# Two graph-attention layers on one core: moving head, value and residual work between VectorE, ScalarE and TensorE

## The chip, the cores and the metric

The kernel runs on one core of a Trainium2 chip. The metric is the device time of one execution in microseconds. Five engines work beside each other, each through its own instruction stream in its own order, and wait for one another by semaphores: TensorE (PE; its weight loads are listed apart as PEld), VectorE (DVE), ScalarE (ACT), GpSimd (POOL) and SyncE (SP), which here only issues transfers.

## The reference, cut to what matters

Sixteen graphs (batches) of N = 1024 nodes with D = 256 features go through two layers; everything is fp32.

```python
# layer 0: 4 heads of 64. With a 0/1 adjacency only edge type 1 exists.
h = x @ W                                   # 4 heads x 64
w = leaky_relu(e_src[i] + e_dst[j]);  w = -1e9 where adj == 0
dst = softmax(w) @ h + bias
out = relu(dst) + h                         # per head
out = (out - mean) / sqrt(var + 1e-6) * ln_gamma + ln_beta   # over the 64 of a head
x = layernorm(x + out)
# layer 1: 8 heads of 32
n = layernorm(x) * gamma1 + beta1
o = softmax(where(adj > 0, n n^T / sqrt(32), -inf)) @ n
x1 = x + o;  y = layernorm(x1) * gamma2 + beta2
x = layernorm(x1 + gelu(y @ W1 + b1) @ W2 + b2)              # 256 -> 1024 -> 256
```

## The kernel before, in words

A batch's 1024 nodes are 8 blocks of 128 rows (`NB`), or two halves of 512 (`NH`, `BPH` = 4 blocks each). Two Python generators, `layer0` and `layer1`, each run over all batches and yield after every step with a cost. A loop at the end of `fast_path` decides which of them makes the next step: `COURSE` says how far layer 0 of the next batch should be while layer 1 of this batch is at a given place, so that layer 0 of batch b+1 is woven into layer 1 of batch b. All of it is decided when the program is built.

Layer 0 of a batch is `prepare` and then `attention0`. `prepare` goes over pairs of blocks: it transposes x (L253), transposes the adjacency (L321) into an 8-bit mask (L322), multiplies x by the weights into a PSUM tile `ph` of 264 columns (L348), and takes from it on ScalarE the exponentials of the attention terms (L349 to L351) and four products of 128x64 that are the values `v0` (L353), and on VectorE the residual `hb` = `ph` + bias (L373). `attention0` has 16 steps a batch: VectorE makes four 128x512 weight tiles (L400), TensorE multiplies them by the values (L415) into an accumulator `av` in PSUM; every two steps one head of one half is complete. The last column of `av` is the softmax's denominator.

`after0` is a chain, a generator whose pieces are given out later, when a clock of step costs reaches them (`begin(chain, wait)`, and `yield` inside the chain for the next wait). `complete(chain)` gives out all that remains at once. For each head the chain divides, applies the ReLU and adds the residual (L444, L447, L456). After the fourth head of a half it does the four heads' norms together on tiles of 128x1024 (L471 to L487, with a square on ScalarE, L477, and a power on GpSimd, L224), then the row norm and layer 1's first norm (`sq` at L240), the residual `x1` (L510), the transposed normed rows `nT` (L253, L259) and the values `v1` (L520). Layer 1's attention needs `nT` and `v1` of both halves.

Layer 1 of a batch is `attention1`, 32 steps of four heads each (scores L543, exponentials L548, mask L554, products with the values L561 and L568), and then `mlp`: per 256 rows eight hidden blocks (L663, GELU at L670), and for each 128 rows the second product (`second`, L676, 16 recorded matmuls in one stretch), followed by the last norm (L706 on). `finish1` stands between the two: it adds the residual, makes the norm and adds `b2` to `x1` (L638, L639).

PSUM has 8 tiles in rotation: four `ps` (scores, hidden blocks, spread factors), two `acc` (`ps_a`: `ph`, `av`, and transposes through `side_bank` while layer 1 is in its attention), two `po`.

Of the kernel before, what the change touches and what calls it, by code (L numbers as in the profile page):

```python
# [39 lines left out]
P = 128  # L40
# [10 lines left out]
def fast_path(  # L51
# [55 lines left out]
    ps_a = ctx.enter_context(tc.tile_pool(name="ps_a", bufs=2, space=PSUM))  # L107
# [63 lines left out]
    for i, (_, _, dst) in enumerate(terms):  # L171
# [10 lines left out]
    nbias0_r = const.tile([P, D], F32, name="nbias0_r")  # L182
    nc.vector.tensor_scalar(nbias0_r, bias0_r, -1.0, None, op0=OP.mult)

    lng0_r, lnb0_r, g1_r, be1_r, b2_r = [
        const.tile([P, D], F32, name=name) for name in ("lng0_r", "lnb0_r", "g1_r", "be1_r", "b2_r")
# [6 lines left out]
    def later_weights():  # L193
        for t, src in ((lng0_r, lng0), (lnb0_r, lnb0), (g1_r, gamma1), (be1_r, beta1), (b2_r, b2)):
            nc.sync.dma_start(t, bass.AP(tensor=src.tensor, offset=src.offset, ap=[[0, P], [1, D]]))
# [7 lines left out]

        nc.vector.tensor_sub(b2_r, b2_r, be1_r)
# [36 lines left out]

    def side_bank(shape):

        if place[1][1] < ATTN1:
            return ps_a.tile(shape, F32, name="acc")
        return ps_s.tile(shape, F32, name="ps")
# [65 lines left out]
    def prepare(b, hb, esr, v0, dinv, mask):  # L312
# [3 lines left out]
        def turn_mask(k):  # L316
            i = b * NB + k
            ak = adj_blocks.pop(i)
            pt = ps_a.tile([P, NB, P], BF16, name="acc")
# [12 lines left out]
        for k in range(0, NB, GB):  # L332
# [12 lines left out]
            for g in range(GB):  # L345
                ph = ps_a.tile([P, D + 2 * H0], F32, name="acc")
# [5 lines left out]
                for hd in range(H0):  # L352
                    nc.scalar.mul(  # L353
                        v0[:, k + g, hd, 0:HO], ph[:, hd * HO : (hd + 1) * HO], v0[:, k + g, hd, HO : HO + 1]
                    )
                begin(take_h(hb[-1][:, (k + g) % BPH, :], ph), 1.5)
# [8 lines left out]
    def turn_sources(dst):  # L365
        es = ps_a.tile([P, GB, P], F32, name="acc")
        for g in range(GB):
            nc.tensor.transpose(es[:, g, :], apart[g].rearrange("p h q -> p (h q)"), ident)
        nc.scalar.copy(dst, es.rearrange("p g q -> p (g q)"))
        yield from ()  # L370

    def take_h(h, ph):
        nc.vector.tensor_add(h, ph[:, 0:D], bias0_r)  # L373
        yield from ()

    def attention0(b, hb, v0, esr, dinv, factors, mask, rinv):
# [51 lines left out]
        for i, (n, hd, j4) in enumerate(steps):  # L428
            if j4 == 0:
                av = ps_a.tile([P, BPH, HO + 1], F32, name="acc")  # L430
# [6 lines left out]
            if j4 == NB - 4:  # L437
                norms[b, n, hd] = after0(b, n, hd, av, hb[n], rinv[:, n * BPH : (n + 1) * BPH, :])
                begin(norms[b, n, hd], 2.5)
            yield 2.0  # L440

    def relu_residual(av, hd, hb, rinv):

        nc.vector.reciprocal(rinv[:, :, hd], av[:, :, HO])  # L444
        t = two.tile([P, BPH, HO], F32, name="relu")
        for q in range(BPH):
            nc.vector.scalar_tensor_tensor(  # L447
                t[:, q, :],
                av[:, q, 0:HO],
                rinv[:, q, hd : hd + 1],  # L450
                nbias0_r[:, hd * HO : (hd + 1) * HO],
                op0=OP.mult,
                op1=OP.max,
            )
        h = hb[:, :, hd * HO : (hd + 1) * HO]
        nc.vector.tensor_add(h, h, t)  # L456

    def after0(b, n, hd, av, o, rinv):


        relu_residual(av, hd, o, rinv)
        if hd < H0 - 1:
            return
        yield 1.5
        heads = [P, BPH * H0, HO]
        rowwise = [P, BPH, D]
        xl = one.tile(rowwise, F32, name="xl")
        load_x(xl, b, n * BPH, BPH)
        oh = o.rearrange("p g (h e) -> p (g h) e", e=HO)
        s = small.tile([P, BPH * H0], F32, name="s0")  # L470
        nc.vector.tensor_reduce(s, oh, axis=mybir.AxisListType.X, op=OP.add)  # L471
        nc.vector.scalar_tensor_tensor(
            oh, s[:, :, None].to_broadcast(heads), -1.0 / HO, oh, op0=OP.mult, op1=OP.add
        )
        yield 2.0
        sq = one.tile(rowwise, F32, name="sq")
        nc.scalar.activation(sq, o, AF.Square)  # L477
        yield 2.5
        v = small.tile([P, BPH * H0], F32, name="v0s")
        nc.vector.tensor_reduce(v, sq.rearrange("p g (h e) -> p (g h) e", e=HO), axis=mybir.AxisListType.X, op=OP.add)  # L480
        nc.vector.tensor_scalar(v, v, 1.0 / HO, EPS_HEAD, op0=OP.mult, op1=OP.add)
        r = power(v, BPH * H0, "r0")
        nc.vector.tensor_mul(o, o, lng0_r[:, None, :].to_broadcast(rowwise))
        nc.vector.tensor_add(xl, xl, lnb0_r[:, None, :].to_broadcast(rowwise))
        yield 3.0
        nc.vector.tensor_mul(oh, oh, r[:, :, None].to_broadcast(heads))
        nc.vector.tensor_add(o, o, xl)  # L487
        yield 2.0
# [17 lines left out]
        yield 2.5  # L506

        x1 = three.tile(rowwise, F32, name="x1")
        for g in range(BPH):
            nc.vector.scalar_tensor_tensor(  # L510
                x1[:, g, :], normed[:, g, :], ratio[:, g : g + 1], be1_r, op0=OP.mult, op1=OP.add
            )
        nT = two.tile([P, DC, HALF], F32, name="nT")
        for g in range(0, BPH, GB):
            transpose_rows(nT[:, :, g * P : (g + GB) * P], normed[:, g : g + GB, :], g1_c, be1_c)
            yield 1.5
        v1 = three.tile([P, BPH, H1, HD + 1], F32, name="v1")
        nc.vector.memset(v1[:, :, :, HD], 1.0)
        for g in range(BPH):
            nc.vector.tensor_mul(  # L520
                v1[:, g, :, 0:HD],
# [723 lines left out]
```

## Time and profile before

| | |
|---|---|
| time, median of 3 | 3648.02 us (3647.32 to 3652.49) |
| profiled span | 3649.4 us |
| PE busy | 3449.4 us, 95% |
| DVE busy | 2988.7 us, 82% |
| ACT busy | 2155.9 us, 59% |
| POOL busy | 384.4 us, 11% |
| first scores of the sixth batch to those of the seventh | 1022.92 to 1247.72 us |

Busy time is the union of an engine's instructions. Matmuls are pipelined and their ends are modelled, so a busy PE may still be a PE that is held up inside a run of matmuls. An fp32 matmul is recorded as two instructions, an fp32 transpose as one. One batch takes about 223 us, of which layer 1's attention takes some 134 us and its MLP some 89 us.

### The profile page before, as it was taken

The numbers are of one execution on the slowest core, as the hardware profiler recorded it, in microseconds if no ns is written. First come the engines' busy times: TensorE is split into PE (matmuls) and PEld (weight loads), VectorE is DVE, ScalarE is ACT, GpSimd is POOL, SyncE is SP. The second block draws the span as 40 slices with busy tenths as digits, with TensorE's granted clock in tenths as the row PEclk, the third lists the DMA queues.
The fourth block names the chain that finished last, engine by engine and source line by source line (L and its number), as shares of the span: only waits on it lengthen the run. The fifth ranks groups of instructions, "written<-read, shape, count | busy, mean of one in ns | idle before, by whom it ended". The sixth has DMA issues, their size and how long they took to land.

```text
span 3649.4 us, 142033 instructions
## 1 busy us (share of the span) xinstructions
PE 3449.4 (95%) x64417; PEld 2302.3 (63%) x64417; DVE 2988.7 (82%) x5332; ACT 2155.9 (59%) x4732; POOL 384.4 (11%) x360
## 2 busy tenths in 40 slices
PE   6699999999999999999999999999999999999998
PEld 5457576675756757566584765757567575665846
DVE  5788887888878888798887978888788887888884
ACT  3564746647475573755738466474664747557464
POOL 0102011010110101101010010101101011010110
PEclk9899999999999999999999999999999999999999
DMA  4100201011020110201102010020201102010000
GB/s 105 35 16 26 36 12 40 13 30 32 14 43 10 34 27 15 44 9 36 23 16 46 8 42 15 26 36 13 41 11 31 31 14 46 7 38 9 15 7 14
DMA packets 77814, 97.55 MB, mean 27 GB/s; under 512 B 9104, under 2 KB 60048, under 8 KB 77200
## 3 DMA queue, kind: packets, MB, share of 16 engines
q0 software_dynamic: 18432, 33.56, 6.5%
q1 hardware_dynamic: 57184, 53.76, 4.8%
q8 instruction: 506, 8.29, 0.9%
q10 hardware_dynamic: 1584, 1.05, 0.1%
q14 instruction: 108, 0.88, 0.1%
HBM read 105.13 MB, written 16.78 MB: 33 GB/s over the span
## 4 chain that ended last, share of the span: by engine, by line
PE 64%; DVE 25%; issue 4%; ACT 3%; POOL 3%; DMA 1%; SPq 0%; ACTq 0%; POOLq 0%; DVEq 0%
PE ps L543 13%; PE po L561 10%; PE ps L663 9%; PE acc L415 9%; DVE p L554 7%; PE po L676 7%; PE po L568 6%; DVE p L400 6%; PE acc L348 3%; POOL r L224 3%; DVE st L229 2%; PE acc L321 1%; PE acc L253 1%; PE ps L389 1%; DVE mv L230 1%
## 5 line engine op out<-in xcount | busy, mean ns | idle before, releaser
L554 DVE TENSOR_TENSOR p<-p,mask 128x1024 f32<-128x1024 f32 x1024 | 1199.3, 1218 | 161.2 <-ACT p L548 157.3
L548 ACT ACTIVATE p<-ps 128x512 f32<-128x512 f32 x2048 | 1059.6, 614 | 331.7 <-PE ps L543 329.9
L543 PE MATMUL ps<-nT 32*128 32x512 f32 x4096 | 770.1, 655 | 12.6 <-ACT cb L391 10.0
L400 DVE SCALAR_TENSOR_TENSOR p<-cb,dinv,mask 128x512 f32<-128x512 f32 x1024 | 698.5, 744 | 0.9 <-ACT cb L391 0.9
L568 PEld LDWEIGHTS po<-v,p 128*32 128x32 f32 x32768 | 389.4, 109 | 335.0 <-issue 239.3
L415 PE MATMUL acc<-v,p 128*64 128x65 f32 x16384 | 556.1, 226 | 42.1 <-DVE p L400 40.1
L415 PEld LDWEIGHTS acc<-v,p 128*64 128x64 f32 x16384 | 512.0, 139 | 114.3 <-DVE p L400 61.6
L670 ACT ACTIVATE hid<-ps,b_sb 128x256 f32<-128x256 f32 x512 | 235.5, 471 | 556.9 <-PE ps L663 556.5
L561 PE MATMUL po<-p,v 128*32 128x512 f32 x2048 | 548.3, 610 | 10.5 <-DVE p L554 8.8
L561 PE MATMUL po<-p,unit 128*32 128x512 f32 x2048 | 547.9, 610 | 0.0
L663 PE MATMUL ps<-yT,w_sb 128*128 128x256 f32 x2048 | 491.0, 387 | 0.4 <-issue 0.4
L676 PE MATMUL po<-w_sb,hid 128*128 128x256 f32 x2048 | 465.0, 381 | 0.0
L676 PEld LDWEIGHTS po<-w_sb,hid 128*128 128x128 f32 x2048 | 385.4, 190 | 64.0 <-issue 11.4
L663 PEld LDWEIGHTS ps<-yT,w_sb 128*128 128x128 f32 x2048 | 375.6, 190 | 64.9 <-issue 13.1
L568 PE MATMUL po<-v,p 128*32 128x33 f32 x32768 | 387.7, 198 | 9.5 <-issue 4.3
L543 PEld LDWEIGHTS ps<-nT 32*128 32x128 f32 x4096 | 268.2, 186 | 171.1 <-issue 56.9
L561 PEld LDWEIGHTS po<-p,v 128*32 128x32 f32 x2048 | 78.6, 109 | 388.3 <-DVE p L554 206.1
L224 POOL TENSOR_TENSOR r<-v,mhalf 128x1 f32<-128x1 f32 (+1 forms) x160 | 158.1, 988 | 1009.1 <-DVE v L710 721.6
L348 PE MATMUL acc<-w0e,xT 128*128 128x264 f32 x512 | 146.4, 409 | 29.5 <-DVE hb L373 20.9
L322 ACT ACTIVATE mask<-acc,shift_c 128x1024 uint8<-128x1024 bf16 x128 | 144.3, 1127 | 43.6 <-PE acc L321 42.8
L304 POOL DMA_DIRECT2D ak<-in_adj_dram x128 | 69.7, 544 | 862.7 <-PE acc L321 840.3
L224 POOL TENSOR_TENSOR r<-v1s,mhalf 128x4 f32<-128x4 f32 x32 | 34.9, 1090 | 1134.6 <-DVE ranges L444 894.6
(117 smaller groups left out, 2927.9 us busy)
## 6 DMA issues: line engine op xcount, KB each, us to landing
ak<-in_adj_dram POOLq DMA_DIRECT2D x128, 256.0 KB, 3.9
xk<-in_x_dram SPq DMA_DIRECT2D x64, 256.0 KB, 2.8
xl<-in_x_dram SPq DMA_DIRECT2D x32, 512.0 KB, 4.0
out_dram<-z SPq DMA_DIRECT2D x128, 128.0 KB, 1.7
w_sb<-in_L_gnn_W_dram SPq DMA_DIRECT2D x2, 1024.0 KB, 8.0
v<-in_L_gnn_a_src_dram SPq DMA_DIRECT2D x2, 320.0 KB, 4.8
v<-in_L_gnn_a_dst_dram ACTq DMA_DIRECT2D x1, 320.0 KB, 5.0
xl<-in_L_gnn_a_dst_dram ACTq DMA_DIRECT2D x1, 320.0 KB, 5.3
```

The source lines that it names most:

```text
L224: nc.gpsimd.tensor_tensor(r, src, mhalf[:, :n], op=OP.pow)
L348: nc.tensor.matmul(ph, xT[:, c, g * P : (g + 1) * P], w0e[:, c, :], start=c == 0, stop=c == DC - 1)
L400: nc.vector.scalar_tensor_tensor(p[:, i, :], cb[:, hd % PAIR, :], dinv[:, j2 + i, hd : hd + 1], mask[n][:, j2 + i, :], op0=OP.max, op1=OP. ...
L415: nc.tensor.matmul(av[at : at + TILE, q, :], ps[i // 2][:, i % 2, q * P + at : q * P + at + TILE], v0[:, j4 + i, hd, :], start=j4 + i == 0 ...
L543: nc.tensor.matmul(tiles[e], of_keys[q, quad, keys], of_queries[q, quad, :], start=True, stop=True)
L548: nc.scalar.activation(p[:, i, :], tiles[e + i], AF.Exp, scale=SCALE1)
L554: nc.vector.tensor_mul(p, p, mask[n][:, jb, None, :].to_broadcast([P, PAIR, HALF]))
L561: nc.tensor.matmul(moved[at * Q : (at + 1) * Q, :], v, ps[0][:, e, :], start=jb == 0, stop=jb == NB - 1)
L568: nc.tensor.matmul(held[at : at + Q, q, e, :], ps[1][:, e, q * P + at : q * P + at + Q], values[:, hd, :], start=jb == 0 and e == 0 and q ...
L663: nc.tensor.matmul(ph, w1_sb[:, c, f * P : (f + 1) * P], yT[:, c, q * P : (q + GB) * P], start=c == 0, stop=c == DC - 1,)
L670: nc.scalar.activation(hid[f // 4][:, f % 4, :], ph, AF.Gelu, bias=b1_sb[:, f : f + 1], scale=1.0)
L676: nc.tensor.matmul(po, hid[f // 4][:, f % 4, g * P : (g + 1) * P], w2_sb[:, f, :], start=f == 0, stop=f == FC - 1,)
```

## The change

1. Layer 0's values. The bias is added to the values (a weighted mean of values plus bias is the mean plus bias), on VectorE for all four heads in two instructions (`values0`: an add and a multiplication by the exponentials). The four ScalarE products go; the residual `hb`, now without the bias, is a ScalarE copy.
2. ReLU. Division and ReLU become four ScalarE activations on the accumulator (`divide0`); VectorE keeps the reciprocal and the residual's addition.
3. Head norms are done for two heads at a time as these get ready, on 128x512, in place of four heads on 128x1024 at the end of a half.
4. Layer 1's residual and values. `x1` is a ScalarE product (four of 128x256 per half). `v1` is no longer computed from the normed rows: `nT`, which already has gamma and beta, is transposed back by TensorE (8 transposes per half) and copied by ScalarE (2 copies of 128x512). As the values now hold beta, it leaves `x1` and `b2`.
5. `b2` is added to `x1` by a chain of its own, later (`add_bias2`).
6. The MLP's second product yields in its middle, so that a layer 0 step may be put there.
7. The two `acc` tiles are chosen by hand (`bank0`): one that an accumulator occupies is left alone, and a tile's readers are given out before it is taken again.
8. `COURSE` lets layer 0 of the next batch be finished 18 instead of 14 cost units before the end of layer 1, and several waits of the chains are shorter.

```diff
+    def bank0(shape, dtype=F32):
+        i = min((i for i in range(2) if not banks0[i]["busy"]), key=lambda i: banks0[i]["taken"])
+        for chain in banks0[i]["readers"]:
+            complete(chain)
...
-                for hd in range(H0):
-                    nc.scalar.mul(
-                        v0[:, k + g, hd, 0:HO], ph[:, hd * HO : (hd + 1) * HO], v0[:, k + g, hd, HO : HO + 1]
-                    )
-                begin(take_h(hb[-1][:, (k + g) % BPH, :], ph), 1.5)
+                bank["readers"] = [values0(v0[:, k + g, :, :], ph)]
+                begin(bank["readers"][0], 1.0)
+                nc.scalar.copy(hb[-1][:, (k + g) % BPH, :], ph[:, 0:D])
...
+    def values0(v, ph):
+        t = two.tile([P, H0, HO], F32, name="z")
+        nc.vector.tensor_add(t.rearrange("p h e -> p (h e)"), ph[:, 0:D], bias0_r)
+        nc.vector.tensor_mul(v[:, :, 0:HO], t, v[:, :, HO : HO + 1].to_broadcast([P, H0, HO]))
...
+    def divide0(av, t, rinv):
+        nc.vector.reciprocal(rinv, av[:, :, HO])
+        yield 0.3
         for q in range(BPH):
-            nc.vector.scalar_tensor_tensor(
-                t[:, q, :],
-                av[:, q, 0:HO],
-                rinv[:, q, hd : hd + 1],
-                nbias0_r[:, hd * HO : (hd + 1) * HO],
-                op0=OP.mult,
-                op1=OP.max,
-            )
+            nc.scalar.activation(t[:, q, :], av[:, q, 0:HO], AF.Relu, scale=rinv[:, q : q + 1])
...
-        x1 = three.tile(rowwise, F32, name="x1")
-        for g in range(BPH):
-            nc.vector.scalar_tensor_tensor(
-                x1[:, g, :], normed[:, g, :], ratio[:, g : g + 1], be1_r, op0=OP.mult, op1=OP.add
-            )
...
+        for g in range(BPH):
+            nc.scalar.mul(x1[:, g, :], normed[:, g, :], ratio[:, g : g + 1])
...
-        for g in range(BPH):
-            nc.vector.tensor_mul(
-                v1[:, g, :, 0:HD],
-                normed[:, g, :].rearrange("p (h e) -> p h e", e=HD),
-                g1_r.rearrange("p (h e) -> p h e", e=HD),
-            )
+        for g in range(0, BPH, GB):
+            pt = side_bank([P, GB, DC, P])
+            for i in range(GB):
+                for c in range(DC):
+                    nc.tensor.transpose(pt[:, i, c, :], nT[:, c, (g + i) * P : (g + i + 1) * P], ident)
+            nc.scalar.copy(
+                v1[:, g : g + GB, :, 0:HD], pt.rearrange("p g c (h e) -> p g (c h) e", e=HD)
+            )
...
+                if f == FC // 2 - 1:
+                    yield 1.75
...
-    COURSE = [(0.0, 1.0), (ATTN1, 1.45), (WORK1 - 14.0, 2.0), (WORK1, 2.0)]
+    COURSE = [(0.0, 1.0), (ATTN1, 1.45), (WORK1 - 18.0, 2.0), (WORK1, 2.0)]
```

## The prediction

> **What bounds the kernel now.** I read the page's busy line first, then the waits of TensorE, then the busy time by stretches of one batch, then the timeline where a wait is long.
>
> ```profile
> PE 3449.4 (95%) x64417; PEld 2302.3 (63%) x64417; DVE 2988.7 (82%) x5332; ACT 2155.9 (59%) x4732; POOL 384.4 (11%) x360
> PE 64%; DVE 25%; issue 4%; ACT 3%; POOL 3%; DMA 1%; SPq 0%; ACTq 0%; POOLq 0%; DVEq 0%
> ```
>
> TensorE is busy 95%: whatever the change does off TensorE can win at most the other 200 us, plus what is hidden in runs of matmuls that are held up but count as busy. But a quarter of the chain that ended last is on VectorE, so TensorE's holes are mostly VectorE's. Who makes the holes, from the waits of TensorE (waiter, whom it waited for, total us, times, longest):
>
> ```profile
> PE acc L253 <- ACT sq L240: 53.4, 17, 11.0
> PE acc L415 <- DVE p L400: 40.1, 21, 5.0
> PE acc L348 <- DVE hb L373: 20.9, 19, 1.1
> PE acc L321 <- ACT xT L256: 13.7, 30, 0.5
> PE ps L543 <- ACT cb L391: 10.0, 15, 0.7
> PE po L561 <- DVE p L554: 8.8, 18, 1.7
> ```
>
> The largest comes once a batch: TensorE stands before the transposes of layer 1's normed rows, at the end of the norm chain of the second half. The next is layer 0's attention without weights from VectorE. Now one batch in six stretches (turn of the batches; attention with `prepare`; attention with `attention0`; three parts of the MLP with `attention0`). After each stretch's length stand busy us of PE, PEld, DVE, ACT and POOL:
>
> ```profile
> 1016.00:1042.00 26.00, 23.27 (x245) 13.09 (x247) 23.36 (x50) 19.16 (x41) 7.96 (x5) 0.96 0.23 57
> 1042.00:1108.00 66.00, 63.96 (x1470) 34.62 (x1462) 47.66 (x59) 53.76 (x140) 4.76 (x8) 0.99 0.25 43
> 1108.00:1156.00 48.00, 46.79 (x1287) 26.27 (x1288) 45.77 (x61) 30.08 (x58) 0.00 (x0) 1.00 0.02 4
> 1156.00:1186.00 30.00, 29.14 (x366) 24.53 (x362) 22.58 (x54) 12.63 (x23) 1.96 (x2) 1.00 0.02 6
> 1186.00:1222.00 36.00, 34.08 (x473) 28.77 (x473) 34.78 (x77) 14.28 (x25) 8.22 (x5) 0.95 0.09 24
> 1222.00:1239.00 17.00, 17.00 (x190) 14.82 (x189) 11.72 (x32) 4.21 (x9) 0.65 (x2) 1.00 0.05 17
> ```
>
> VectorE is full at 1108 to 1156 (95%) and 1186 to 1222 (97%), and 90% at the turn; ScalarE is loaded only beside `prepare` (81%). PE idles 8.8 us of these 223. Counting from start to start of successive matmul records, with the usual tight spacing of each kind taken off, I get some 14 us of holes a batch. The extra is held-up runs such as the first below: 8 transposes in 1.92 us, where 128 of them elsewhere take 21.0 us.
>
> ```profile
> 1037.14 2.08 ACT L240 ACTIVATE sq<-hb,t,r 128x256 f32<-128x256 f32 x4 [1.05 <-DVE t L234]
> 1037.29 0.42 DVE L373 TENSOR_TENSOR hb<-acc,bias_r 128x256 f32<-128x256 f32 x1
> 1037.79 1.92 PE L253 MATMUL acc<-ident,sq 128*128 128x128 f32 x8 [2.28 <-ACT sq L240]
> ```
>
> [...] in the timeline at 1032 to 1039 us the norm chain's small VectorE operations stand between the 1.2 us mask operations. [...] L373 only reads `ph`, yet waits 74.0 us in total for ScalarE's L353, which reads it as well. So in the new code VectorE's read of `ph` still comes after ScalarE's.
>
> **The change part by part.** Durations are from the rows of these lines.
>
> ```profile
> L447 DVE SCALAR_TENSOR_TENSOR relu<-acc,ranges,nbias_r 128x64 f32<-128x64 f32 x512 | 109.9, 277 | 4.5
> L373 DVE TENSOR_TENSOR hb<-acc,bias_r 128x256 f32<-128x256 f32 x128 | 54.1, 422 | 74.0 <-ACT v L353 74.0
> L510 DVE SCALAR_TENSOR_TENSOR x<-sq,ratio,be_r 128x256 f32<-128x256 f32 x128 | 57.9, 480 | 2.4 <-ACT sq L240 1.3
> L520 DVE TENSOR_TENSOR v<-sq,g_r 128x256 f32<-128x256 f32 x128 | 44.6, 410 | 0.0
> L353 ACT ACTIVATE v<-acc,v 128x64 f32<-128x64 f32 x512 | 118.7, 315 | 0.0
> ```
>
> VectorE loses these four rows, 109.9 + 54.1 + 57.9 + 44.6 = 266.5 us. It gains 128 adds and 128 multiplications of 128x256 in `values0`, 256 x 0.42 (L373's) = 107 us. Five 128x1024 operations of the head norms become two of 128x512 each: 1218 ns at 1024 (L483) and 425 at 256 (L456) give 161 ns fixed, so 5 x 32 x 0.16 = 26 us, and 5 more for the second small one (L481). Net 266.5 - 107 - 31 = 128 us less, 8 a batch, of 187. By place: beside `prepare` 8 x 0.42 = 3.4 us more, where VectorE has 18 us free; at the turn and around 1210 us 3.2 us less each (four L510 and four L520); in `attention0` 0.86 us less per head; `b2`'s addition leaves the full stretch at 1102 to 1108 us (1.2 us).
>
> ScalarE loses L353's 118.7 us and gains 512 ReLUs of the same shape and source (118.7), 128 copies of 128x256 (0.371 as L369: 47), 128 products for `x1` (L240's, with two scalar operands, are 0.52 back to back; L369's copy is 0.37; I take 0.45: 58), 64 value copies of 128x512 (0.594 as L256: 38), and about 5 for halved squares. Net about 148 us, to 2304 us or 64%. Beside `prepare`, where it is fullest, it loses 8 x (4 x 0.232 - 0.371) = 4.5 us and gets `x1` and `v1` of one half, 3.0 us: no new bound. The rest falls where it is 30 to 63% busy.
>
> TensorE gains 256 transposes. L253's groups on `o` cost 21.0/128 = 0.16 and 19.2/128 = 0.15 us each: 38 to 42 us, and no matmul goes. The order of instructions has 112 more runs of equal instructions on TensorE, 64 of them these transposes; the other 48 come from the split second product, and a change of kind costs about 0.1 to 0.2 us (309 instead of 216 ns from start to start): 5 to 10 us. I take 48 us, 3.0 a batch. This is on the path without anything to hide it.
>
> New waits: the ReLUs stand in ScalarE's queue and wait for VectorE's reciprocal; behind them queue GELUs, and behind these TensorE for a `ps` tile. Each step fills two of four `ps` tiles, so a delay under one step (some 3.6 us) is hidden, and the reciprocal comes after at most four L400 (2.7 us). The `acc` tile of a finished head now waits for VectorE and then ScalarE, 0.18 + 4 x 0.23 = 1.1 us against 1.04 before. Both at nothing in my case, 1 us a batch each at worst.
>
> What comes back, per batch. The turn holds TensorE some 4.9 us (2.28 + 1.0 of held-up transposes, the rest in waits for masks). The chain gets shorter: the last head norm runs on half the elements (the power takes 2.07 in place of 3.82 us, as L224's rows for 8 and 16 elements; four VectorE operations 0.5 us less each, the square 0.45), layer 0 ends 4 units earlier, and in the new order the four `sq` stand before the first exponentials of the next batch instead of after the masks of the third step. That is over 8 us; I count 4.0 us saved. In the full stretch 1186 to 1222 the holes are 1.9 us idle and 2.0 in held-up runs; two to four heads' ReLUs and the 3.2 us go, but the 18 in `COURSE` squeezes 22 attention steps into 38 units instead of 42: 2.5 saved. At 1102 to 1156: 1.0. At 1156 to 1186: 0.3. The waits for `xT`, `cb` and `hb` stay. Sum 7.8 saved, 3.0 paid: 4.8 us a batch, 77 for 16, and 3 us at the start, where layer 0 runs alone. 3648 - 80 = 3568 us.
>
> **The rivals.**
> - VectorE is the true pace of three of the six stretches and nearly all holes close: 11 saved, 3 paid, 8 x 16 = 128, 3520 us. For: 25% of the chain. Against: `prepare`'s waits are untouched.
> - The squeeze by `COURSE` and reciprocals before ReLUs give back half: 4.5 saved, 3 paid, 24 us, 3624 us. For: VectorE at 97% in the very stretch that is squeezed.
> - TensorE bound: its 48 us stay, and the freed VectorE time is slack, with 1 to 2 us of new waits at ScalarE: 3 + 1.5 paid, 3 saved, about 1.5 x 16 = 24 us slower, 3672 us. For: PE at 95% busy. Against: a TensorE bound alone would not show 40.1 and 53.4 us of waits.
>
> **How the numbers follow.** The main case 0.48, nearly all holes 0.19, half given back 0.17, slower 0.16. The likeliest is 3568 us. The range 3505 to 3650 reaches just below the second case and to no change; it leaves out most of the slower case and the far end of the second, 2 in 10. Faster by over 0.2%: 0.48 + 0.19 + 0.14 = 0.81; within 0.2%: 0.03 + 0.01 = 0.04; slower 0.15.
>
> **What would show it.** In the changed profile: VectorE near 2860 and ScalarE near 2300 us; the rows of transposes back about 40 us; TensorE's wait for `sq` from 53.4 to under 15, and for layer 0's weights from 40.1 to under 25; the wait for VectorE's read of `ph` still about 20. I am wrong if TensorE's idle time stays near 200 us, or if a new wait of TensorE for a `ps` tile behind GELU, or of an `acc` tile behind the ReLU, stands over 20 us.

## The result: 1.2% slower, and the profile after

| | before | after |
|---|---|---|
| time, median of 4 | 3650.26 us (3647.32 to 3654.28) | 3695.07 us (3689.25 to 3704.23) |
| profiled span | 3649.4 us | 3702.3 us |
| mean granted TensorE clock | 0.985 | 0.978 |

The ratio is 1.0124 with an interval of 1.01 to 1.0149: 45 us slower, where 80 us faster was forecast. The time lies above the whole range.

The page's busy line and the first line of the chain that ended last, of the changed kernel:

```profile
PE 3487.3 (94%) x64673; PEld 2358.5 (64%) x64673; DVE 2857.4 (77%) x4882; ACT 2274.1 (61%) x5084; POOL 410.2 (11%) x392
PE 76%; DVE 16%; ACT 6%; issue 2%; DMA 0%; POOL 0%; ACTq 0%; POOLq 0%; DVEq 0%
```

Work moved as intended: VectorE lost 131 us and its share of the chain fell from 25% to 16%. But TensorE is busy 38 us longer, and its idle time has not shrunk: 3702.3 - 3487.3 = 215 us, after 200 before. The waits of TensorE in the changed kernel (waiter, whom it waited for, total us, times, longest) say why:

```profile
PE acc L421 <- DVE p L406: 63.4, 36, 3.2
PE acc L327 <- DVE z L378: 50.5, 15, 3.4
PE ps L559 <- ACT cb L397: 17.2, 30, 0.9
PE acc L327 <- ACT xT L262: 13.7, 30, 0.5
PE acc L259 <- ACT sq L236: 11.9, 2, 9.2
```

The turn of the batches is repaired: the wait for `sq` (now L236) fell from 53.4 to 11.9 us. In its place stand layer 0's attention without weights (L421 for L406), 63.4 us instead of 40.1, and a wait that is new in this size: the mask's transposes (L327) for VectorE's read of `ph` (L378), 50.5 us in 15 pieces of up to 3.4 us, once a batch.

Split by stage, from layer 1's first scores of a batch to its first hidden block and from there to the next batch's first scores, means over the third to the fifteenth batch (worked out from the starts in the trace):

| us per batch | attention | MLP |
|---|---|---|
| before | 133.5 | 89.3 |
| after | 132.7 | 93.4 |

The profiled execution of the changed kernel is the longest of its four, 9 us above the median, or some 0.6 us a batch. Attention gained 0.7 us and the MLP lost 4.1. So most of the loss is beside the MLP, while what attention should have gained is nearly all eaten up within it.

**The loss beside the MLP.** The waits of VectorE in the changed kernel have a line that had no counterpart:

```profile
DVE hb L467 <- ACT relu L459: 152.6, 104, 3.0
```

And the timeline of the changed kernel shows what one of these does (start, length, engine, line, operation, in brackets the idle time before it and its releaser):

```profile
1171.51 1.22 DVE L653 TENSOR_TENSOR x<-x,o 128x1024 f32<-128x1024 f32 x1
...
1172.64 0.18 DVE L456 RECIPROCAL ranges<-acc 128x4 f32<-128x4 f32 x1
1172.85 0.93 ACT L459 ACTIVATE relu<-acc,ranges 128x64 f32<-128x64 f32 x4 [3.45 <-DVE ranges L456]
1173.82 0.42 DVE L467 TENSOR_TENSOR hb<-hb,relu 128x256 f32<-128x256 f32 x1 [1.00 <-ACT relu L459]
1174.28 0.69 DVE L477 TENSOR_REDUCE s<-hb 128x8 f32<-128x512 f32 x1
1175.00 0.69 DVE L478 SCALAR_TENSOR_TENSOR hb<-s,hb 128x512 f32<-128x512 f32 x1
1175.61 2.73 DVE L406 SCALAR_TENSOR_TENSOR p<-cb,dinv,mask 128x512 f32<-128x512 f32 x4
...
1176.40 2.67 PE L421 MATMUL acc<-v,p 128*64 128x65 f32 x64 [1.85 <-DVE p L406]
```

VectorE makes the reciprocal, stands still for 1.00 us while ScalarE does the four ReLUs, then adds. Layer 0's next weights (L406) queue behind that add and behind two operations of the head norms, and TensorE waits 1.85 us for the first of them. In 82 of 128 heads the add directly follows the reciprocal on VectorE, and in 15 more only four small operations stand between, so little fills the gap. The four ReLUs themselves take 0.93 us; on the mean over the heads they begin 1.1 us after the reciprocal ends, mostly because other work stands ahead of them in ScalarE's queue. About 40 us later in the same batch it happens again (1.39 us on VectorE, 1.64 us on TensorE). Loads of function tables on ScalarE are not behind this: the trace has 92 of them, 118.0 us, in both kernels.

**The loss inside attention.** The timeline of the changed kernel a little earlier:

```profile
1104.09 1.23 DVE L646 TENSOR_TENSOR o<-o,x 128x1024 f32<-128x1024 f32 x1
...
1105.27 0.75 PE L584 MATMUL po<-v,p 128*32 128x33 f32 x64
...
1107.61 0.17 DVE L651 TENSOR_SCALAR v1s<-mv 128x4 f32<-128x4 f32 x1
1107.69 1.22 DVE L653 TENSOR_TENSOR x<-x,o 128x1024 f32<-128x1024 f32 x1
...
1108.82 0.41 DVE L378 TENSOR_TENSOR z<-acc,bias_r 128x256 f32<-128x256 f32 x1
...
1109.38 0.61 PE L327 MATMUL acc<-identb,ak 128*128 128x128 bf16 x8 [3.37 <-DVE z L378]
```

The first piece of `finish1` occupies VectorE from 1104.09 to 1108.91, and the change put `x1 += o` (L653, 1.22 us) at its end, where it used to be in the second piece. The read of `ph`, L378, stands behind that piece. The mask's transposes now take the `acc` tile that L378 reads, so TensorE stops for 3.37 us. Before, TensorE ran these transposes (there L321) in this place and met the late read (L373) only at L348, for 1.13 us:

```profile
1101.05 0.62 PE L321 MATMUL acc<-identb,ak 128*128 128x128 bf16 x8
...
1102.32 0.42 DVE L373 TENSOR_TENSOR hb<-acc,bias_r 128x256 f32<-128x256 f32 x1
...
1102.80 1.16 PE L348 MATMUL acc<-w0e,xT 128*128 128x264 f32 x4 [1.13 <-DVE hb L373]
```

**What a hole costs besides itself.** Stretches of the changed kernel around the same hole one batch later (start and end, length, then busy us of PE, PEld, DVE, ACT and POOL, the granted clock, the DMA share and GB/s):

```profile
1329.50:1332.90 3.40, 1.03 (x72) 0.63 (x60) 3.19 (x11) 1.51 (x4) 0.53 (x1) 1.00 0.00 0
1332.90:1339.70 6.80, 5.80 (x28) 2.79 (x32) 6.65 (x10) 2.67 (x8) 2.00 (x2) 0.50 0.28 39
1339.80:1343.20 3.40, 3.40 (x125) 1.72 (x118) 2.53 (x3) 2.36 (x6) 0.00 (x0) 1.00 0.02 5
```

After a stretch with TensorE busy for 1.03 of 3.40 us, its clock is 0.50 for 6.8 us: L327's eight transposes then take 1.01 us instead of 0.61, L354's four matmuls 2.07 instead of 1.11.

```profile
1333.89 1.01 PE L327 MATMUL acc<-identb,ak 128*128 128x128 bf16 x8 [3.37 <-DVE z L378]
1334.70 2.07 PE L354 MATMUL acc<-w0e,xT 128*128 128x264 f32 x4
```

Not every hole costs this: of the 15 holes before L327, five run into such a half-clock stretch, and the one at 1109 us does not. Length times (1 - granted clock), summed over the span, is 55.4 us before and 82.2 us after. Up to 27 of the 53 us between the two profiled spans may therefore be TensorE at half clock, counted as busy. This is a bound and not a measured share: part of a half-clock stretch is idle or waits anyway. Two executions of the changed kernel point the same way: one of 3687.3 us has a granted clock of 0.982, the profiled one of 3702.3 us 0.978, and 0.004 of the clock is 15 us of the span; that the two go together doesn't show which makes which. Nor are holes the whole reason: nine half-clock stretches of 3.41 us, some 15 us by the same measure, follow a stretch with only 0.37 us of idle time (last section).

### The profile page after: what moved, and what is told of

It is laid out like the page before. It is cut to its first block, busy times and chain, and to the rows that moved or that the text cites. A ratio compares the mean times of both kernels' runs of the same rounds, so it can differ in the third digit from the quotient of the medians.

```text
span 3702.3 us, 142339 instructions
## 1 busy us (share of the span) xinstructions
PE 3487.3 (94%) x64673; PEld 2358.5 (64%) x64673; DVE 2857.4 (77%) x4882; ACT 2274.1 (61%) x5084; POOL 410.2 (11%) x392
## 4 chain that ended last, share of the span: by engine, by line
PE 76%; DVE 16%; ACT 6%; issue 2%; DMA 0%; POOL 0%; ACTq 0%; POOLq 0%; DVEq 0%
PE ps L559 17%; PE po L577 13%; PE acc L421 11%; PE po L696 9%; PE ps L682 8%; PE po L584 7%; DVE p L406 3%; PE acc L354 3%; DVE st L225 2%; PE acc L259 2%; PE acc L327 2%; DVE p L570 1%; ACT relu L459 1%; DVE mv L226 1%; DVE o L646 1%
## 5 line engine op out<-in xcount | busy, mean ns | idle before, releaser
L570 DVE TENSOR_TENSOR p<-p,mask 128x1024 f32<-128x1024 f32 x1024 | 1202.7, 1220 | 245.1 <-ACT p L564 240.7
L564 ACT ACTIVATE p<-ps 128x512 f32<-128x512 f32 x2048 | 1071.1, 632 | 286.3 <-PE ps L559 283.2
L559 PE MATMUL ps<-nT 32*128 32x512 f32 x4096 | 761.7, 648 | 24.4 <-ACT cb L397 17.2
L406 DVE SCALAR_TENSOR_TENSOR p<-cb,dinv,mask 128x512 f32<-128x512 f32 x1024 | 698.4, 744 | 6.8 <-ACT cb L397 6.8
L421 PE MATMUL acc<-v,p 128*64 128x65 f32 x16384 | 575.6, 228 | 71.4 <-DVE p L406 63.4
L421 PEld LDWEIGHTS acc<-v,p 128*64 128x64 f32 x16384 | 526.6, 141 | 148.3 <-DVE p L406 71.8
L584 PEld LDWEIGHTS po<-v,p 128*32 128x32 f32 x32768 | 396.4, 110 | 321.1 <-issue 238.0
L577 PE MATMUL po<-p,v 128*32 128x512 f32 x2048 | 550.7, 613 | 2.4 <-DVE p L570 2.4
L577 PE MATMUL po<-p,unit 128*32 128x512 f32 x2048 | 550.0, 613 | 0.0
L696 PE MATMUL po<-w_sb,hid 128*128 128x256 f32 x2048 | 480.0, 385 | 0.0
L584 PE MATMUL po<-v,p 128*32 128x33 f32 x32768 | 390.2, 198 | 4.2 <-issue 3.3
L577 PEld LDWEIGHTS po<-p,v 128*32 128x32 f32 x2048 | 78.4, 108 | 371.6 <-DVE p L570 202.0
L220 POOL TENSOR_TENSOR r<-v,mhalf 128x1 f32<-128x1 f32 (+1 forms) x160 | 148.5, 928 | 756.8 <-DVE v L732 304.2
L220 POOL TENSOR_TENSOR r<-v1s,mhalf 128x4 f32<-128x4 f32 x32 | 61.9, 1933 | 1171.5 <-DVE v1s L651 1171.5
L459 ACT ACTIVATE relu<-acc,ranges 128x64 f32<-128x64 f32 x512 | 119.1, 323 | 109.2 <-DVE ranges L456 109.2
L236 ACT ACTIVATE z<-z,t,r 128x256 f32<-128x256 f32 x128 | 81.6, 638 | 162.2 <-DVE t L230 160.7
```

Source lines behind the costliest of these rows:

```text
L220: nc.gpsimd.tensor_tensor(r, src, mhalf[:, :n], op=OP.pow)
L406: nc.vector.scalar_tensor_tensor(p[:, i, :], cb[:, hd % PAIR, :], dinv[:, j2 + i, hd : hd + 1], mask[n][:, j2 + i, :], op0=OP.max, op1=OP. ...
L421: nc.tensor.matmul(av[at : at + TILE, q, :], ps[i // 2][:, i % 2, q * P + at : q * P + at + TILE], v0[:, j4 + i, hd, :], start=j4 + i == 0 ...
L459: nc.scalar.activation(t[:, q, :], av[:, q, 0:HO], AF.Relu, scale=rinv[:, q : q + 1])
L559: nc.tensor.matmul(tiles[e], of_keys[q, quad, keys], of_queries[q, quad, :], start=True, stop=True)
L564: nc.scalar.activation(p[:, i, :], tiles[e + i], AF.Exp, scale=SCALE1)
```

## The experiments

They were run in five groups, each with the kernel before beside it, whose median was 3650.2 to 3654.5 us; a ratio is to that one, with its 95% interval. A difference between two kernels of different groups is therefore good to some 4 us. The edits are to the changed kernel unless said otherwise, and each run has a short name (e1 to e18) with its result.

**Which part costs the MLP its 4 us: the ReLU on ScalarE?**

Back to VectorE, with two instructions in place of four activations and an add:

```diff
-        yield 0.3
-        for q in range(BPH):
-            nc.scalar.activation(t[:, q, :], av[:, q, 0:HO], AF.Relu, scale=rinv[:, q : q + 1])
+        nc.vector.tensor_mul(t, av[:, :, 0:HO], rinv[:, :, None].to_broadcast([P, BPH, HO]))
...
-        nc.vector.tensor_add(h, h, t)
+        nc.vector.scalar_tensor_tensor(h, t, 0.0, h, op0=OP.max, op1=OP.add)
```

> The changed kernel with part 2 put back to VectorE in another form: one product of the accumulator with the reciprocals (128x256) and one instruction for ReLU and residual (128x256), no ScalarE activation. VectorE gains 128 x 0.42 = 54 us of work and loses its wait of 152.6 us; ScalarE loses 119 us. Theory (the wait for ScalarE costs more than the work saved): the time falls by 30 to 60 us. Rival (VectorE's work is what matters, its waits are slack): the time rises by 5 to 30 us.

e3: 3641.53 us, ratio 0.9965 [0.9951, 0.9979]: 54 us under the changed kernel (58 by the ratios), and slightly faster than before. The MLP stretch is back at 89.3 us. TensorE's waits in this kernel:

```profile
PE acc L327 <- DVE z L378: 50.5, 15, 3.4
PE acc L421 <- DVE p L406: 32.6, 21, 4.4
```

The wait for weights halved while VectorE is busy 54 us more (2911.6), and the other hole is untouched. So VectorE's work was not what counted here. Either its standing still did, or the ReLUs in ScalarE's queue, which are gone as well; e5 below keeps them there and parts the two.

The same swap in the kernel before, which has none of the other edits; both forms leave layer 0's bias out of the ReLU. First only the ScalarE form, then the two VectorE instructions:

```diff
-            nc.vector.scalar_tensor_tensor(
...
+            nc.scalar.activation(t[:, q, :], av[:, q, 0:HO], AF.Relu, scale=rinv[:, q, hd : hd + 1])
```

> The kernel before the change with division and ReLU as four ScalarE activations, reciprocal and residual on VectorE as in the changed kernel, in the place and order of before (the ReLU leaves out layer 0's bias, which has no place in the activation). Theory (VectorE stands still between reciprocal and addition, whatever else is changed): VectorE waits over 100 us for the ReLU, and the time rises by 20 to 60 us although VectorE has 110 us less to do. Rival (only together with the two-head norms and the squeezed pace): within 10 us of before, or faster.

```diff
-        for q in range(BPH):
-            nc.vector.scalar_tensor_tensor(
...
+        nc.vector.tensor_mul(t, av[:, :, 0:HO], rinv[:, :, hd : hd + 1].to_broadcast([P, BPH, HO]))
...
-        nc.vector.tensor_add(h, h, t)
+        nc.vector.scalar_tensor_tensor(h, t, 0.0, h, op0=OP.max, op1=OP.add)
```

> The kernel before the change with division and ReLU in two VectorE instructions of 128x256 (0.42 us each) in place of four of 128x64 and an addition (1.28 us) per head (the ReLU leaves out layer 0's bias). VectorE's work falls by 128 x 0.43 = 55 us, no wait is added. Theory (VectorE's work in layer 0's attention holds TensorE up): 10 to 35 us faster than before. Rival (TensorE bound): within 7 us.

3675.06 us, 1.0062 [1.0045, 1.0079], for the ScalarE form (e15); 3641.25 us, 0.9964 [0.995, 0.9978], for the two instructions (e16). VectorE's waits in the first:

```profile
DVE hb L449 <- ACT relu L447: 201.4, 128, 5.8
```

Taking 110 us of work off VectorE alone makes the kernel before 22 us slower, with VectorE waiting 201 us for the result. The two forms are 34 us apart here and 54 in the changed kernel. The mechanism is thus the edit's own and needs none of the other edits, but its size depends on them: the MLP stretch is 90.3 us here (e15) and 93.4 in the changed kernel. Part of e3's gain (some 12 us by e16) is that two instructions of 128x256 beat four of 128x64 and an add.

**Can the add simply come later?** First by its due time, then far later, with buffers for it:

```diff
-                begin(norms[b, n, hd], 3.8)
+                begin(norms[b, n, hd], 5.0)
```

> The changed kernel, with the residual's addition begun 5.0 instead of 3.8 units after a head is complete, so that the four weight tiles of the next step stand between the reciprocal and the addition in VectorE's queue. Work is the same. Theory (VectorE stands still behind its own reciprocal until ScalarE's ReLUs are done, and layer 0's weights queue behind it): VectorE's wait for the ReLU falls from 152.6 us to under 30, TensorE's wait for the weights from 63.4 to under 35, and the time falls by 20 to 50 us. Rival (VectorE had time to lose, the pace of layer 0 and the split product are what costs): VectorE's wait falls, TensorE's wait for the weights stays above 50, and the time moves by under 10 us. If the later addition delays the norm chain instead, the wait of TensorE for sq rises above 30 us.

```diff
-                t = two.tile([P, BPH, HO], F32, name="relu")
+                t = three.tile([P, BPH, HO], F32, name="relu")
-                begin(norms[b, n, hd], 3.8)
+                begin(norms[b, n, hd], 5.7)
-        sq = one.tile([P, BPH, PAIR * HO], F32, name="sq")
+        sq = one.tile([P, BPH, PAIR * HO], F32, name="sqh")
```

> The changed kernel with the residual's addition begun 5.7 instead of 3.8 units after the head, which now puts two to four large VectorE instructions between the reciprocal and the addition for 112 of 128 heads (the earlier run with 5.0 did so for 52, after 31 in the changed kernel itself); the square of the head norms has a buffer of its own and the ReLU's output a third one, without which the order would lock. Work is the same, and the ReLUs stay on ScalarE. Theory (what costs is VectorE standing still behind ScalarE's ReLU): VectorE's wait for the ReLU falls from 152.6 us to under 50, and the time by 25 to 50 us, most of what moving the ReLU to VectorE won. Rival (what costs is the ReLUs in ScalarE's queue, which hold up the GELUs behind them until the reciprocal is there): VectorE's wait falls and the time by under 12 us.

The first (e2), 3693.29 us, 1.0108 [1.0091, 1.0125], tells little: in 60 of 128 heads the add still follows the reciprocal directly (82 in the changed kernel), and VectorE still waits 131 us for the ReLU. The second (e5), 3695.73 us, 1.0125 [1.0098, 1.0151], tells more than its time. Its waits:

```profile
DVE hb L467 <- ACT relu L459: 47.0, 30, 2.6
PE acc L421 <- DVE p L406: 36.5, 21, 4.2
```

The MLP stretch fell to 89.8 us, though the ReLUs are still on ScalarE. But attention rose to 136.2, 3.5 us a batch. Filling the gap repairs the MLP stretch, as the theory says, and the time is all given back in attention. What takes the 3.5 us is not settled; seen are waits of TensorE's transposes back for `nT` (10.6 us) and more idle time of VectorE in front of the last norm.

The buffer `sqh` alone, which e5 and two more kernels have:

```diff
-        sq = one.tile([P, BPH, PAIR * HO], F32, name="sq")
+        sq = one.tile([P, BPH, PAIR * HO], F32, name="sqh")
```

> The changed kernel with a buffer of its own for the square of the head norms and nothing else: what three earlier runs had in common. In all three layer 1's attention took 134.6 to 136.2 us of a batch, against 132.7 in the changed kernel. Theory (the buffer, by taking a wait away, lets the chain's transposes and copies be put where TensorE then waits for them): attention near 134.9 us, MLP near 93.4, about 30 us slower than the changed kernel. Rival (the three edits do it, each in its own way): within 8 us of the changed kernel.

e9: 3697.44 us, 1.0129 [1.0113, 1.0146]: no effect, so the lengthening of attention in e5 is due to the later add or to the ReLU's third buffer, which had no run of its own.

**The pace, the split product, the transposes back.** Each undone, the first two with `sqh`:

```diff
-    COURSE = [(0.0, 1.0), (ATTN1, 1.45), (WORK1 - 18.0, 2.0), (WORK1, 2.0)]
+    COURSE = [(0.0, 1.0), (ATTN1, 1.45), (WORK1 - 14.0, 2.0), (WORK1, 2.0)]
```

> The changed kernel with COURSE at 14 units before the end again (and the square's own buffer, without which the order would lock). Theory (the pace is not what costs): within 10 us of the changed kernel. Rival (squeezing layer 0 into 38 units instead of 42 is what makes the MLP stretch longer): the time falls by 20 to 60 us, the MLP's 93.4 us of a batch to about 90.

```diff
-                if f == FC // 2 - 1:
-                    yield 1.75
...
-            yield 1.75
+            yield 3.5
```

> The changed kernel with the MLP's second product in one piece again (and the square's own buffer). Theory: 5 to 10 us less from fewer changes of kind on TensorE, so at most 12 us either way. Rival (the break puts layer 0's steps too close together for VectorE): the time falls by 20 to 50 us and TensorE's wait for the weights from 63.4 us to under 45.

```diff
-        for g in range(0, BPH, GB):
-            pt = side_bank([P, GB, DC, P])
...
+        for g in range(BPH):
+            nc.vector.tensor_mul(
...
```

> The changed kernel with part 4 undone: values and residual of layer 1 by VectorE from the normed rows again, no transposes back (256 fewer on TensorE, 102 us more on VectorE, 102 us less on ScalarE). Theory (the transposes are an addition to the bound engine without anything in return): the time falls by 25 to 45 us. Rival (VectorE's 102 us are worth more than TensorE's 39): the time rises by 10 to 60 us.

- The old pace (e7): 3688.51 us, 1.0107 [1.009, 1.0124]. The MLP stretch falls to 90.7 us, attention rises to 134.6, and the total hardly moves. VectorE's wait for the ReLU grows to 236.9 us, yet TensorE's for weights shrinks to 37.9: the squeeze decides how much of VectorE's standing still reaches TensorE. Some 2 to 3 of the MLP's 4.1 us need both the squeeze and the ReLU on ScalarE (e3 has the squeeze alone, and none of the loss), but taking the squeeze back costs attention some 2 us a batch.
- The second product in one piece (e8): 3767.54 us, 1.032 [1.0303, 1.0337], 73 us slower. TensorE's wait for weights grows to 90.0 us. The split, which the prediction booked as a cost, is a large gain beside the change's other parts.
- The values by VectorE again (all of part 4 undone, e4): 3690.88 us, 1.01 [1.0083, 1.0117]. TensorE is busy 29.5 us less and VectorE 89 us more, and the time is the same within the intervals.

**The hole before the mask's transposes: the tile, the read, or the sum ahead of it?** First other choices of the tile:

```diff
-        i = min((i for i in range(2) if not banks0[i]["busy"]), key=lambda i: banks0[i]["taken"])
+        i = min((i for i in range(2) if not banks0[i]["busy"]), key=lambda i: (any(item[1] is c for item in chains for c in banks0[i]["readers"]), banks0[i]["taken"]))
```

> The changed kernel, but the hand-written choice of the acc tile prefers one whose readers have already been given out; nothing else differs. Theory (a tile is taken whose reader, the values' addition, stands behind the first norm of layer 1 in VectorE's queue): the wait of TensorE's mask transposes for the values' addition goes from 50.5 us to under 15, and the time falls by 30 to 50 us, to about 3650. Rival (VectorE is late there anyway, and TensorE meets the same addition one instruction later, as it did before the change at the product of x with the weights): that wait comes back as 20 to 45 us at the product, and the time falls by under 15 us.

e1: 3699.64 us, 1.0117 [1.0101, 1.0134], and the wait still 50.5 us. The read had already been given out when the tile is chosen, so the new key chose as before, and the run doesn't answer its question.

```diff
-        i = min((i for i in range(2) if not banks0[i]["busy"]), key=lambda i: banks0[i]["taken"])
+        i = min((i for i in range(2) if not banks0[i]["busy"]), key=lambda i: (len(banks0[i]["readers"]), banks0[i]["taken"]))
...
-        nc.vector.tensor_add(x1, x1, o)
         yield 2.0
+        nc.vector.tensor_add(x1, x1, o)
```

> The changed kernel with two small things undone: the acc tile is chosen so that one with a VectorE or ScalarE reader of its own is taken last (the choice of the first run fell on the same tiles as before, as the reader had been given out already), and the sum of x1 and o stands in the second piece of layer 1's norm chain again, not in its first. Theory (a tile whose reader stands behind 4.7 us of norm work is taken too early): the mask transposes' wait of 50.5 us goes, the product of x with the weights waits 15 to 30 us in its place, and the time falls by 18 to 30 us. Rival (the attention is paced by ScalarE and VectorE, and TensorE's hole there is filled from elsewhere): waits change and the time moves by under 8 us.

e6: 3917.35 us, 1.0732 [1.0714, 1.075], the worst of all. TensorE's waits in it:

```profile
PE acc L354 <- ACT mask L328: 110.5, 82, 1.6
PE acc L421 <- DVE p L406: 56.1, 51, 3.2
PE acc L372 <- ACT xT L262: 32.7, 48, 0.8
```

The wait for L378 is gone. But the list of readers leaves out ScalarE's read for the mask, so a tile that this read still holds counts as free, and masks, products and transposes pile onto one tile. Three more kernels do not count a side transpose as a taking of the tile, and have `x1 += o` later as above; the second has the VectorE ReLU too, the third also 16 for 18 in `COURSE`:

```diff
-            return bank0(shape)[0]
+            old = [bank["taken"] for bank in banks0]
+            tile, bank = bank0(shape)
+            bank["taken"] = next(t for b, t in zip(banks0, old) if b is bank)
+            return tile
```

> The changed kernel with the sum of x1 and o in the second piece of layer 1's norm chain again, and with tiles of side transposes not counted as a taking, so that after them the mask takes the same acc tile once more, as it did in the kernel before; masks and products otherwise alternate as they do in the changed kernel (the earlier try let all masks fall on one tile). Theory: the mask transposes' wait of 50.5 us goes, the product with the weights waits 15 to 30 us in its place, the time falls by 18 to 30 us. Rival (the hole is filled from elsewhere): the time moves by under 8 us.

> The two edits of the run before and, besides, division and ReLU on VectorE in two instructions of 128x256. If the two losses are apart, as theory has it, the gains add up: 54 and some 20 us less than the changed kernel, about 3620. If they share a cause, about 3640, no better than the ReLU on VectorE alone.

> The run before with COURSE at 16 units before the end, half of the way back. Theory (with VectorE relieved of its wait the pace no longer matters): within 8 us of the run before. Rival (layer 0 squeezed into fewer units still leaves TensorE without weights, 32.6 us of waits in the run with the ReLU on VectorE): 10 to 30 us less.

3747.23 us for e10 (1.0266 [1.0249, 1.0283]), 3690.83 for e11 (1.0108 [1.0091, 1.0125]) and 3743.99 for e12 (1.0257 [1.024, 1.0274]). The mask's wait goes, and the side transposes take its place (in e10 L375 for `xT` 32.7 us, L539 for `v1` 31.6). With two tiles, each rule tried here that keeps one stage from a late reader puts another stage behind one. Leave the tiles, then, and bring the reader forward:

```diff
-                begin(bank["readers"][0], 1.0)
+                begin(bank["readers"][0], 0.5)
```

> The changed kernel with the values' addition begun 0.5 instead of 1.0 units after the product, so that it stands ahead of the first piece of layer 1's norm chain in VectorE's queue; which tile is taken stays as it is. Theory: the mask transposes' wait goes from 50.5 us to under 10 with nothing in its place, attention 2 to 3 us a batch shorter, time 30 to 50 us less. Rival (VectorE, begun earlier, stands still behind ScalarE's copy of the same tile, and its masks come later): the wait goes, VectorE's wait for the copy rises from 32 us to over 70, the time moves by under 12 us.

e13: 3697.4 us, 1.0125 [1.0108, 1.0142]: nothing gained. L327's wait is gone; instead the product with the values waits for masked exponentials (L577 for L570, 38.2 us), since L378 now stands at the head of VectorE's queue while ScalarE still reads the tile (278.6 us of waits for L360, from 31.9; most of these only stood elsewhere, since VectorE's wait for L564 falls from 240.7 to 58.7). So the sum ahead of it, later, without the early read and with the VectorE ReLU:

```diff
         r = power(v, BPH, "r1")
-        nc.vector.tensor_add(x1, x1, o)
         yield 2.0
+        nc.vector.tensor_add(x1, x1, o)
```

> The changed kernel with ReLU on VectorE and the sum of x1 and o in the second piece of the norm chain; the values' addition where the change put it. Theory (the hole before the mask transposes shortens from 3.4 to 2.2 us, 15 times, but stays): 18 to 25 us less than the ReLU on VectorE alone, near 3620, and 10 to 15 us more than all three. Rival (the sum alone is what counted): as fast as all three, within 6 us of 3607. Second rival (only both together): within 8 us of 3641.

e18: 3618.05 us, 0.9906 [0.989, 0.9923]: 23 us under the VectorE ReLU alone, for moving one addition of 1.22 us.

```profile
PE acc L327 <- DVE z L378: 33.5, 15, 2.2
PE acc L421 <- DVE p L406: 25.4, 36, 4.2
```

Against e3 the wait for L378 fell by 17.0 us and the one for weights by 7.2: the sum of a batch's second half had stood ahead of weights too (1171.51 us in the timeline above).

**The VectorE ReLU, the later sum and the earlier read together (the edits of e3, e18 and e13), and once more with part 4 undone as well:**

> The run before it, and ReLU and division on VectorE in two instructions, and the sum of x1 and o in the second piece of the norm chain. If the losses are apart: the 54 us of the ReLU and those of the first run added, near 3600. If only the ReLU counts: 3635 to 3645.

> The version with values early, sum later and ReLU on VectorE, with part 4 undone besides: values and residual of layer 1 by VectorE, 256 transposes less on TensorE (38.5 us busy), 102 us more on VectorE. Theory (with the holes gone TensorE's work is the bound): 20 to 40 us faster, near 3575. Rival (VectorE's 102 us make new holes[...]): 5 to 50 us slower than 3607.

e14: 3607.12 us, 0.9877 [0.9861, 0.9894], and e17: 3610.55 us, 0.9878 [0.9862, 0.9895]. The first is the best kernel here, 1.2% faster than before. Its busy line:

```profile
PE 3432.1 (95%) x64673; PEld 2310.0 (64%) x64673; DVE 2892.4 (80%) x5010; ACT 2169.6 (60%) x4572; POOL 393.1 (11%) x392
```

and its waits of TensorE (L576, L569 and L583 here are L577, L570 and L584 of the changed kernel):

```profile
PE po L576 <- DVE p L569: 38.9, 32, 1.3
PE acc L421 <- DVE p L406: 27.2, 38, 4.2
PE po L583 <- DVE o L625: 15.2, 16, 1.0
PE acc L259 <- ACT sq L236: 11.3, 1, 11.3
```

Most waits that remain are short: the once-a-batch holes of 3.4 us are gone. L576's wait came with the early read, as in e13, and is about as long in all as L327's was in e18; but the lost clock, 46.8 us in e18, is 28.3 here. The granted clock is 0.992, and the lost clock was 82.2 us in the changed kernel. TensorE has the same 64673 matmul records as there and is busy 55 us less, so those 55 us were not added work but matmuls at half clock or held up. Attention takes 130.8 us a batch and the MLP 89.3. Undoing part 4 leaves the time as it is, now in a kernel without the large holes: attention gets 1.0 us a batch shorter, the MLP 1.1 longer.

## Why the prediction was wrong, point by point

- **Sizes of the work: right.** VectorE 2857.4 us (near 2860 forecast), ScalarE 2274.1 (near 2300), the transposes back 38.5 us in their two rows (38 to 42).
- **The turn of the batches: right.** The wait for `sq` is 11.9 us (under 15). e14, which keeps this part, takes 2.7 us a batch less than before in attention.
- **"New waits: ... Both at nothing in my case, 1 us a batch each at worst": the step that failed.** It followed ScalarE's queue (ReLU behind reciprocal, GELUs behind, TensorE for `ps`) and the `acc` tile behind the ReLU. Neither wait came: the trace shows none for `ps` behind GELU, and 2.3 us behind the ReLU. It did not follow VectorE's queue: the residual's addition needs the ReLU, VectorE waits for it 152.6 us in all, and layer 0's weights queue behind the addition. The prediction asked only on ScalarE's side of the exchange who stands behind a waiting instruction. On VectorE's side the trace shows it: in the 1.00 us before 1173.82 nothing behind the addition ran. Measured, the ReLU on ScalarE costs 22 us by itself (e15 against before), and 34 us (e15 against e16) to 54 us (changed kernel against e3) beside the two VectorE instructions. The prediction had the two new waits at 0, at most 32 us together, and 2.8 us a batch saved in the MLP's stretches, which lost 4.1.
- **"The waits for `xT`, `cb` and `hb` stay": wrong for the last two.** The read of `ph` went from 20.9 us (L348) to 50.5 (L327); the wait of the scores for `cb` went from 10.0 to 17.2. For `ph` the order of instructions would have shown both causes: L653 in `finish1`'s first piece and the mask's transposes on the other `acc` tile. Moving the sum gave 23 us (e18), the earlier read 11 more (e14), and nothing by itself (e13).
- **The transposes back, "on the path without anything to hide it", 3.0 us a batch: wrong.** TensorE's busy time fell by 29.5 us without them (e4), but the time by 4 us there (9 by the ratios, within the intervals) and not at all in e17. In e17, without them, attention gains 1.0 us a batch and the MLP, with VectorE's work in their place, loses 1.1.
- **The split product, 5 to 10 us of cost: wrong in sign.** Undoing it costs 73 us (e8).
- **The forecast of closing holes** took each saving from its stage and left the clock out. In the changed kernel 27 us more of clock were lost, by the bound above, in part after new holes.
- **Its signs of being wrong.** TensorE's idle time near 200 us came (215). The other two, waits over 20 us for a `ps` tile behind GELU or an `acc` tile behind the ReLU, did not: they looked at TensorE behind ScalarE, not behind VectorE.
- **The rivals.** The squeeze by `COURSE` by itself is not the cause (e7): it needs the ReLU on ScalarE, and the total stays when it is undone. The slower case came near the time (3672 us) by another way, which is luck: it had TensorE's added 48 us as the loss, and new waits of 1 to 2 us at ScalarE. The waits came, at VectorE, and the time is the same without the transposes that make up most of the 48 us.

With the ReLU back on VectorE and the two orders mended, the rest of the change makes the kernel faster: e14 is 46 us under before, of 80 forecast, with some 12 of it from a form of the ReLU that the change doesn't have (e16). Open stay the exact share of the clock, what lengthens attention in e5, why the early read helps only with the other two edits, what parts 1, 3 and 5 are worth by themselves (no run undoes them alone), and whether some rule for the two tiles beats the early read.

## What to carry to other kernels

Work that goes from engine A to engine B and whose result comes back to A at once is not taken off A here: A waits for B's queue and for the work itself (1.1 and 0.93 us a head on the mean), and the instructions behind the waiting one stood still with it (1.00 us in front of the addition at 1173.82, then 1.85 us of TensorE). Price the round trip, with who is queued behind it, before the instruction that is saved. And look for an operation that moved from one piece of a chain to another: a 1.2 us addition in the wrong piece cost 23 us here, because a PSUM tile's last reader, and some of layer 0's weights, stood behind it.

## What the runs showed of the hardware

The granted clock has two values in the traces of before and of the changed kernel, 1.00 and 0.50. The stretches at 0.50, 24 before and 36 after, are 3.41 us long or a multiple of it, but for the last one of each trace. What sets them off is not settled here. In the changed kernel the holes of 1.64 and 1.84 us in front of layer 0's attention (L421) were followed by half clock in 7 and 5 batches of 15 and not in the others, and nine times a stretch with 0.37 us of idle time was. One of these nine (columns as above):

```profile
1117.90:1121.30 3.40, 3.03 (x14) 0.93 (x14) 3.40 (x6) 3.40 (x9) 0.00 (x0) 1.00 0.00 0
1121.30:1124.70 3.40, 3.40 (x80) 2.02 (x72) 3.40 (x5) 0.56 (x2) 0.00 (x0) 0.50 0.00 0
```

TensorE is busy 3.03 of 3.40 us in the first, with 14 matmuls, and the second runs at half clock. No run here tested why.
